# Two convolutional attention layers with group norm on one core: group statistics through small transfers, and a look-ahead that stops at the last phase

## Chip, core and metric

The kernel runs on one core of a Trainium2 chip, in one launch, in fp32 throughout. The metric is the device time in microseconds (us), the median of several executions. Lines such as L428 are lines of the kernel before; the changed kernel has other numbers for the same statements.

## What is computed

Two layers are applied to x of shape (4, 256, 64, 64), each with a residual and each on a group norm of its input. The group norm has 32 groups of 8 channels; each group of one image gets one mean and one variance.

```python
def _gn(v, G=32, eps=1e-5):
    g = v.reshape(B_, G, C_ // G, H_, W_)
    m = jnp.mean(g, axis=(2, 3, 4), keepdims=True)
    s = jnp.var(g, axis=(2, 3, 4), keepdims=True)
    return ((g - m) / jnp.sqrt(s + eps)).reshape(v.shape)
...
x = x + _L0_conv_ref(_gn(x), ...)
x = x + _L1_conv_ref(_gn(x), ...)
```

Layer 0 ("A" in the kernel) is attention with 8 heads of 32 channels, 4096 queries per image and 1024 keys, which come from 2x2 convolutions with stride 2. Layer 1 ("B") is attention within four areas of 1024 positions per image, plus a depthwise 7x7 convolution of the values, plus a 1x1 projection.

## The kernel before

The work is cut into eight blocks: A for the four images, then B for the four images. A block has 16 units (8 chunks of 512 queries times 2 sets of four heads), a unit has 8 steps (128 keys each). The loop at the end of the function goes through 683 **phases**; a phase does one and a half steps. In each phase TensorE makes score products (tile s, L428), ScalarE takes three exponentials of 128x1024 (L469 twice, L480 once, tile p), TensorE multiplies the previous phase's exponentials with the values (tile av, L494), and VectorE adds them up into the tile acc (L504). Tile p has 6 buffers.

All other TensorE work is **side work**: the products for q, k, v, the projection (all through the helper at L167), the convolution (L1048) and the divisors (tile den, L513). It is cut into **parts** by `yield` in generators. A task, made by `task` or `task_at`, says how many parts it has and when it is due. In each phase the loop decides how many parts to put between the scores and the value products: 0, 1, 2 or, when things are late, 4. The decision uses `pressure()` (parts over the time that is left) and `supply()`, a forecast of how many parts per phase will be at hand. `supply()` looks 24 phases ahead, and spreads what it finds at a rate of 13/16 of a phase. Two queues of instructions are of interest besides: GpSimd's, which also issues the small DMAs of the divisors (few, recs, rb: L527, L535, L537), and SP's, which issues all large DMAs. The order on every engine is the one that this Python loop emits; no other scheduler changes it.

Group norm statistics come from `bn_stats` as chunks pass by. When an image's last chunk has been seen, `plan_norm` does the following for its key (`("A", b)` or `("B", b)`): `aggregate` gives mean and variance of each channel, one channel per partition (L346). `means` multiplies them on TensorE by a 128x128 matrix gmat that averages within groups of 8 partitions (tile gm, L351), ScalarE copies the result out (L352), VectorE forms the deviations (L353 to L355). `variances` does a second such product (tile gv, L359), ScalarE adds eps (L360), GpSimd takes the power -0.5 (L363) and makes the shift (L367, L368). Outside the prologue `means` and `variances` don't run at once: `soon` puts them into a queue `quick`, and the loop takes one from it in a phase in which no side work is under way, no unit ends, and none was taken in the two phases before.

```python
        elif quick and not begun() and not cut and f < PHASES and f > quick_at[0] + 2:
            quick.popleft()()
            quick_at[0] = f
        else:
            if rate > 2:
                parts = side_parts(4)
```

So a phase that takes a group product takes no side work: the branches exclude each other. The normalizations that use the result (`normalize`, L390 and L392) are held back until four phases after it was issued (`after`, `known`).

After the last phase the loop drains what is left: the last units' divisors (their reciprocals go from few through a DRAM tile recs into rb), the last projections `project` and `project_last` (tile ops, L167, taken out by L831 and L859 into xm), and the output DMAs (L834, L860). Outside of the prologue every side product takes the same PSUM bank, `ps_side`.

Of the kernel before, what the change touches and what calls it, by code (L numbers as in the profile page):

```python
# [9 lines left out]
FP = mybir.dt.float32  # L10
I32 = mybir.dt.int32
AF = mybir.ActivationFunctionType
ALU = mybir.AluOpType
AX = mybir.AxisListType

P = 128
B, C, HH, WW = 4, 256, 64, 64
N = HH * WW
CT = C // P
# [19 lines left out]
EPS = 1e-5  # L39
# [21 lines left out]
def direct_path(  # L61
# [122 lines left out]
    plan = {}  # L184

    def at(g, j, f):
        g, j = g + int(j // NKT), int(j % NKT)
        plan.setdefault((g, j), []).append(f)

    side, quick, quick_at = deque(), deque(), [-9]
    now, last = [-1], len(BLOCKS) * UNITS * NKT

    phase = [0]
# [17 lines left out]

    def supply():

        far = 24
        comes = [0] * (far + 1)
        chained = 0
        for parts, _, started, ready, _ in side:
            if started or ready is None or ready():  # L220
                comes[0] += parts
            elif ready.__name__ == "chained":
                chained += 5
                comes[min(chained, far)] += parts
            else:
                comes[1] += parts
        for when, parts in upcoming:
            if when - phase[0] <= far:
                comes[max(when - phase[0], 1)] += parts
        total, least = 0, 4.0  # L230
        for h in range(far):
            total += comes[h]
            least = min(least, total / max(1, (h + 1) * 13 / 16))
        return least

    def choose():
# [35 lines left out]
    def begun():  # L272
        return bool(side) and side[0][2]
# [39 lines left out]

        return ready

    def soon(f):

        if now[0] < 0:
            f()
        else:  # L320
            quick.append(f)

    stats, norms = {}, {}

    def stats_of(key):
# [4 lines left out]
    def keep_busy(n):  # L330
        ps = ps_pair("idle")[:, 0, :P]
        for _ in range(n):
            T.matmul(ps, lhsT=idle, rhs=idle, start=True, stop=True)

    def plan_norm(key, g, j):

        name = f"{key[0]}{key[1]}"
        made = {}

        def aggregate():  # L340
            for tag, cols in (("mv", 2), ("gmean", 1), ("dev", 1), ("gvar", 1)):
                shape = [P, CT, cols] if cols > 1 else [P, CT]
                made[tag] = pool.tile(shape, FP, tag=tag, name=f"{tag}_{name}", bufs=2)
            mv = made["mv"]
            for t in range(CT):
                V.bn_aggr(out=mv[:, t, :], in_=stats[key][:, t].rearrange("p c s -> p (c s)"))  # L346

        def means():
            mv, mean, dev = made["mv"], made["gmean"], made["dev"]
            ps = ps_side(f"gm_{name}")[:, :CT]  # L350
            T.matmul(ps, lhsT=gmat, rhs=mv[:, :, 0], start=True, stop=True)  # L351
            S.copy(mean, ps)  # L352
            V.tensor_sub(dev, mv[:, :, 0], mean)  # L353
            V.tensor_mul(dev, dev, dev)
            V.tensor_add(dev, dev, mv[:, :, 1])  # L355

        def variances():
            ps = ps_side(f"gv_{name}")[:, :CT]
            T.matmul(ps, lhsT=gmat, rhs=made["dev"], start=True, stop=True)  # L359
            S.activation(made["gvar"], ps, AF.Identity, bias=eps)  # L360
            norm = pool.tile([P, 2, CT], FP, tag="norm", name=f"norm_{name}", bufs=8)
            shift, rstd = norm[:, 0, :], norm[:, 1, :]
            G.tensor_tensor(rstd, made["gvar"], neghalf, ALU.pow)  # L363
            if key == ("A", 0):
                V.scalar_tensor_tensor(shift, made["gmean"], -1.0, rstd, ALU.mult, ALU.mult)
            else:
                G.tensor_tensor(shift, made["gmean"], rstd, ALU.mult)  # L367
                G.tensor_scalar(shift, shift, -1.0, None, ALU.mult)  # L368
            norms[key] = shift, rstd
            known[key] = phase[0] if now[0] >= 0 else -4  # L370

        def quietly(f, n):
            f()
            if key == ("A", 0):
                keep_busy(n)

        if key == ("A", 0):
            at(g - 1, 0, lambda: keep_busy(44))
        at(g, j, aggregate)
        at(g, j + (2 if g >= 0 else 1), lambda: soon(lambda: quietly(means, 4)))  # L380
        at(g, j + (6 if g >= 0 else 3), lambda: soon(lambda: quietly(variances, 10)))

    def normalize(key, dst, src, t, by_vector=False):
        while key not in norms:
            while begun():
                advance()
            quick.popleft()()
        shift, rstd = norms[key]
        if by_vector:
            V.tensor_scalar(dst, src, rstd[:, t : t + 1], shift[:, t : t + 1], ALU.mult, ALU.add)  # L390
            return
        S.activation(dst, src, AF.Identity, bias=shift[:, t : t + 1], scale=rstd[:, t : t + 1])  # L392
# [763 lines left out]
        task(parts, g, *args, due=0.6)  # L1156
    f = step = 0
    before, credit = [], 0.0
    while f < PHASES or before or plan or side or quick or norms_left or to_add or to_divide:
        now[0], phase[0] = step, f  # L1160
        exps = scores(f) if f < PHASES else [lambda: None] * 3
        mine = []
        if f < PHASES:
            full, half = parts_of(f)
            mine = sorted(([half] if half else []) + [(full, None)], key=lambda b: b[0])
        due = bool(to_divide)
        exps[0]()
        add_ready()
        due = bool(to_divide) if f >= PHASES else due
        exps[1]()  # L1170
        cut = boundary(before)
        for s, u in before[:cut]:
            accumulate(s, u)
        if cut:
            copies[0] += 1
        _, rate = pressure()
        parts = done_den = 0
        wanted = credit + max(min(supply(), 2.0), min(rate, 2.0))
        bare = cut and not begun() and not due and f < PHASES and rate <= 1.5 and (wanted < 0.8 or not choose())
        if cut and not bare:  # L1180
            evict(before[0][0] // NKT)
        exps[2]()
        if bare:
            evict(before[0][0] // NKT)
            banks.reverse()
            credit = min(wanted, 0.5)
        elif due and not begun():
            done_den = 1
            copies[0] += 1
            g = to_divide.popleft()  # L1190
            divisors(g, *([last - 1] if g == final else []))
            if g < final:
                divide(g, units[g])
            else:
                rb = pool.tile([P, CH], FP, tag="p", name="rb", bufs=PB)
                V.reciprocal(rb, dens[g])
                spare.extend((dens.pop(g), rb))
        elif quick and not begun() and not cut and f < PHASES and f > quick_at[0] + 2:
            quick.popleft()()
            quick_at[0] = f  # L1200
        else:
            if rate > 2:
                parts = side_parts(4)
            elif rate > 1.5 or due or f >= PHASES or wanted >= (0.8 if cut else 1.5):
                parts = side_parts(2)
            elif begun() and side[0][0] % 2:
                parts = side_parts(1)
            elif boundary(mine):
                parts = side_parts(2) if wanted >= 0.9 else 0
            elif wanted >= 0.5 and not cut or begun():  # L1210
                parts = side_parts(1)
            credit = max(-0.5, min(wanted - parts, 0.5))
        for s, u in before[cut:]:
            accumulate(s, u)
        add_ready()
        if f >= PHASES:
            side_parts(2)
        if quick and f >= PHASES:
            quick.popleft()()
        while step < -(-3 * (f + 1) // 2):  # L1220
            do(*divmod(step, NKT))
            step += 1
        for _ in range(3):
            load_share()
        if before:
            evict(before[-1][0] // NKT, True)
        work = max(parts, done_den)
        force = f >= PHASES or f < 20 or pressure()[0] <= 4
        while norms_left and (force or busy(work, 0.75) <= 0.3 + 0.1 * len(norms_left)) and norm_next():
            copies[0] += 1  # L1230
            force = f >= PHASES
        behind[0], copies[0] = min(busy(work), 0.4), 0
        if before:
            evict(before[-1][0] // NKT)
        before = mine
        to_add.extend((s, n) for s, u in mine for n in ((0, 1) if u is None else (2 + u,)))
        f += 1
# [597 lines left out]
```

## Time and profile before

| what | us |
|---|---|
| median of 3 executions (3064.57 to 3065.95) | 3065.22 |
| the profiled execution, its own time | 3063.53 |
| its span from first to last instruction | 3061.5 |
| prologue, to the first score product of the loop | 72.06 |
| 682 phases, from the first to the last phase's first score product | 2961.4 |
| last phase and drain, to the end of the span | 28.1 |

The profiled execution is 1.7 us under the median. TensorE's granted clock was 0.998. In the profile PE is TensorE, PEld its weight loads, DVE is VectorE, ACT is ScalarE, POOL is GpSimd, SP is SyncE; a line of the timeline gives start in us, length in us, engine, source line, operation, what is written from what, and how many instructions were merged; in brackets stands the engine's idle time before it and what ended it. An fp32 matmul of the program shows as two records.

### The profile page before, as it was taken

The numbers are of one execution on the slowest core, as the hardware profiler recorded it, in microseconds if no ns is written. First come the engines' busy times: TensorE is split into PE (matmuls) and PEld (weight loads), VectorE is DVE, ScalarE is ACT, GpSimd is POOL, SyncE is SP. The second block draws the span as 40 slices with busy tenths as digits, with TensorE's granted clock in tenths as the row PEclk, the third lists the DMA queues.
The fourth block names the chain that finished last, engine by engine and source line by source line (L and its number), as shares of the span: only waits on it lengthen the run. The fifth ranks groups of instructions, "written<-read, shape, count | busy, mean of one in ns | idle before, by whom it ended". The sixth has DMA issues, their size and how long they took to land.

```text
span 3061.5 us, 108320 instructions
## 1 busy us (share of the span) xinstructions
PE 3032.8 (99%) x47254; PEld 1280.0 (42%) x47254; DVE 2526.2 (83%) x2769; ACT 2455.9 (80%) x2988; POOL 433.8 (14%) x794
## 2 busy tenths in 40 slices
PE   9999999999999999999999999999999999999998
PEld 6444434444344444333444444444434444443332
DVE  3788988889887787878888888788878888888888
ACT  3888888888887888888888877788777787878885
POOL 0011111111111111111111111111111111111111
PEclk9999999999999999999999999999999999999999
DMA  5244533466354557777866677667755565553232
GB/s 191 51 101 98 126 92 73 109 142 165 83 140 133 143 152 175 189 161 194 204 175 162 156 176 185 152 171 178 176 127 145 144 159 143 149 139 79 50 71 62
DMA packets 644250, 422.73 MB, mean 138 GB/s; under 512 B 409740, under 2 KB 552572, under 8 KB 643768
## 3 DMA queue, kind: packets, MB, share of 16 engines
q1 hardware_dynamic: 619384, 380.11, 49.3%
q0 software_dynamic: 24384, 35.62, 5.1%
q8 instruction: 373, 6.11, 0.9%
q14 instruction: 109, 0.89, 0.1%
HBM read 317.28 MB, written 97.05 MB: 135 GB/s over the span
## 4 chain that ended last, share of the span: by engine, by line
PE 91%; DMA 3%; DVE 2%; ACT 2%; issue 2%; SPq 1%; POOL 0%; DVEq 0%; ACTq 0%; POOLq 0%
PE s L428 31%; PE av L494 26%; PE k0ps L167 4%; PE den L513 4%; PE v0ps L167 4%; PE q1ps L167 4%; PE k1ps L167 4%; PE conv_ps L1048 4%; PE q0ps L167 4%; PE ops L167 4%; PE vals_ps L167 3%; DVE acc L504 1%; ACT p L469 1%; DMA vals<-vout 1%; DMA rows<-vals 1%
## 5 line engine op out<-in xcount | busy, mean ns | idle before, releaser
L504 DVE TENSOR_TENSOR acc<-acc,p 128x1024 f32<-128x1024 f32 x1790 | 2117.4, 1220 | 382.7 <-PE av L494 285.7
L469 ACT ACTIVATE p<-s 128x1024 f32<-128x1024 f32 x1194 | 1159.8, 1025 | 419.3 <-PE s L428 407.6
L480 ACT ACTIVATE p<-s 128x1024 f32<-128x1024 f32 x598 | 619.8, 1036 | 1.5 <-DVE acc L504 0.7
L428 PE MATMUL s<-q,k_A 32*64 32x256 f32 (+1 forms) x10928 | 541.1, 494 | 4.1 <-ACT p L469 3.5
L428 PE MATMUL s<-q,k_B 32*64 32x512 f32 (+1 forms) x10912 | 537.1, 494 | 2.8 <-ACT p L469 2.4
L494 PE MATMUL av<-p,v_A 128*32 128x256 f32 (+1 forms) x4784 | 451.4, 486 | 0.0
L494 PE MATMUL av<-p,v_B 128*32 128x512 f32 (+1 forms) x4776 | 449.4, 487 | 0.0
L428 PEld LDWEIGHTS s<-q,k_B 32*64 32x64 f32 x10912 | 266.0, 130 | 325.1 <-PE s L428 60.4
L428 PEld LDWEIGHTS s<-q,k_A 32*64 32x64 f32 x10928 | 263.2, 130 | 329.1 <-PE s L428 58.5
L537 POOL DMA_DIRECT2D rb<-recs x508 | 251.4, 501 | 510.3 <-DMA recs<-few 497.9
L535 POOL DMA_DIRECT2D recs<-few x127 | 71.3, 561 | 1719.9 <-DVE sums L534 1600.3
L494 PEld LDWEIGHTS av<-p,v_B 128*32 128x32 f32 x4776 | 149.2, 110 | 264.5 <-issue 238.3
L494 PEld LDWEIGHTS av<-p,v_A 128*32 128x32 f32 x4784 | 149.5, 110 | 227.5 <-issue 186.0
L469 ACT ACTIVATE acc<-s 128x1024 f32<-128x1024 f32 x172 | 167.0, 1023 | 80.6 <-PE s L428 80.2
L513 PE MATMUL den<-acc,ones 128*32 128x512 f32 x1024 | 138.5, 605 | 0.9 <-DVE xm L831 0.9
L167 PE MATMUL ops<-cv,wp_sb 128*32 128x512 f32 x1024 | 126.6, 605 | 4.7 <-DVE xm L831 3.5
L527 POOL DMA_DIRECT2D few<-den_sb x127 | 90.5, 713 | 271.9 <-ACT den_sb L526 271.3
L167 PE MATMUL vals_ps<-hv,wqkv_sb 128*32 128x512 f32 x1024 | 124.9, 598 | 0.5 <-issue 0.5
L167 PE MATMUL q1ps<-h,wqkv_sb 128*32 128x512 f32 x1024 | 124.9, 599 | 0.0
L167 PE MATMUL k1ps<-h,wqkv_sb 128*32 128x512 f32 x1024 | 123.0, 597 | 1.7 <-ACT cout L1059 0.9
L167 PE MATMUL q0ps<-hq,wq_sb 128*32 128x512 f32 x1024 | 124.0, 597 | 0.1
L167 PE MATMUL k0ps<-taps,wkv 128*32 128x256 f32 x2048 | 123.9, 383 | 0.0
(102 smaller groups left out, 2089.5 us busy)
## 6 DMA issues: line engine op xcount, KB each, us to landing
rows<-vals SPq DMA_DIRECT2D x384, 195.9 KB
rb<-recs POOLq DMA_DIRECT2D x508, 64.0 KB, 3.6
share<-vals SPq DMA_DIRECT2D x128, 195.9 KB
vala<-vout SPq DMA_DIRECT2D x128, 144.0 KB
vals<-vout SPq DMA_DIRECT2D x128, 144.0 KB
vc<-vala SPq DMA_DIRECT2D x64, 288.0 KB
band<-mats SPq DMA_DIRECT2D x96, 176.0 KB
hq<-in_x SPq DMA_DIRECT2D x32, 512.0 KB
```

The source lines that it names most:

```text
L167: T.matmul(out[cols, :], lhsT=lhsT[:, cols], rhs=rhs, start=start, stop=stop)
L428: T.matmul(out[n : n + WIDE], lhsT=unit[2]()[rows, unit[0], j * P + n : j * P + n + WIDE], rhs=unit[1]()[rows, cols], start=True, stop=True,)
L469: S.activation(p, (a, b)[n], AF.Exp, scale=SCALE)
L480: S.activation(p, c.rearrange("p b (l n) -> p b l n", l=2), AF.Exp, scale=SCALE)
L494: T.matmul(out, lhsT=v[:, j, unit[0] * P + HD * h : unit[0] * P + HD * h + HD], rhs=rhs, start=(j == 0 and not u), stop=(j == NKT - 1), sk ...
L504: V.tensor_add(to, to, p)
L513: T.matmul(dens[g][HD * h : HD * h + HD, :], lhsT=ones, rhs=p(h), start=(n == 0), stop=(n == len(sets) - 1),)
L527: G.dma_start(few[:, 0, :], den_sb[0:P:HD, :].rearrange("h (q n) -> h q n", n=CH // HD))
L535: G.dma_start(recs.rearrange("h (q n) -> (h q) n", n=CH // HD), few[:, 1, :])
L537: G.dma_start(rb[HD * h : HD * h + HD, :], recs[h : h + 1, :].to_broadcast([HD, CH]))
L1048: T.matmul(ps[HD * m : HD * m + HD, (2 * k + i) * size : (2 * k + i + 1) * size].rearrange("p (y x) -> p y x", y=NY), lhsT=band[:, half].r ...
```

## The change

For all keys but the first (`("A", 0)`, in the prologue), the two products, the two copies and the deviations go. In their place `gather` issues two DMAs on GpSimd's queue that bring mean and variance of each channel from one channel a partition to one group a partition (a tile of 32 partitions with 8 channels x 2 values); `of_groups` lets VectorE take the statistics of the 8 means, and the sum of the 8 variances; `scatter` makes scale and shift in five small GpSimd operations, and two more DMAs bring them back to every channel's partition. The steps are issued at fixed steps of the plan (1, 5 and 6 steps after `aggregate`; 1, 2 and 3 in the prologue), not through `quick`, which goes with its branch of the loop. The tile norm has 4 buffers in place of 8. `supply()` no longer looks beyond the last phase, and spreads at 14/16 in place of 13/16.

```diff
-    side, quick, quick_at = deque(), deque(), [-9]
+    side = deque()
...
-        far = 24
+        far = max(1, min(24, PHASES - phase[0]))
...
-            least = min(least, total / max(1, (h + 1) * 13 / 16))
+            least = min(least, total / max(1, (h + 1) * 14 / 16))
...
+        def gather():
+            by_group = made["by_group"] = pool.tile([CT * NG, 8, 2], FP, tag="by_group", name=f"by_group_{name}", bufs=1)
+            for t in range(CT):
+                G.dma_start(by_group[t * NG : (t + 1) * NG], made["mv"][:, t, :])
+
+        def of_groups():
+            by_group = made["by_group"]
+            for tag, cols in (("spread", 6), ("of_means", 2), ("within", 1), ("scale", 2)):
+                made[tag] = pool.tile([CT * NG, cols], FP, tag=f"group_{tag}", name=f"{tag}_{name}", bufs=1)
+            V.bn_stats(out=made["spread"], in_=by_group[:, :, 0])
+            V.bn_aggr(out=made["of_means"], in_=made["spread"])
+            V.tensor_reduce(made["within"], by_group[:, :, 1], AX.X, ALU.add)
+
+        def scatter():
+            scale, within, of_means = made["scale"], made["within"], made["of_means"]
+            shift, rstd = scale[:, 0:1], scale[:, 1:2]
+            G.tensor_scalar(within, within, 0.125, EPS, ALU.mult, ALU.add)
+            G.tensor_tensor(within, within, of_means[:, 1:2], ALU.add)
+            G.tensor_tensor(rstd, within, neghalf[: CT * NG, 0:1], ALU.pow)
+            G.tensor_tensor(shift, of_means[:, 0:1], rstd, ALU.mult)
+            G.tensor_scalar(shift, shift, -1.0, None, ALU.mult)
+            norm = pool.tile([P, CT, 2], FP, tag="norm", name=f"norm_{name}", bufs=4)
+            for t in range(CT):
+                G.dma_start(norm[:, t, :], scale[t * NG : (t + 1) * NG].unsqueeze(1).to_broadcast([NG, 8, 2]))
+            norms[key] = norm[:, :, 0], norm[:, :, 1]
             known[key] = phase[0] if now[0] >= 0 else -4
...
-        at(g, j + (2 if g >= 0 else 1), lambda: soon(lambda: quietly(means, 4)))
-        at(g, j + (6 if g >= 0 else 3), lambda: soon(lambda: quietly(variances, 10)))
+        if by_products:
+            at(g - 1, 0, lambda: keep_busy(44))
+            for n, f, more in ((1, means, 4), (3, variances, 10)):
+                at(g, j + n, f)
+                at(g, j + n, lambda more=more: keep_busy(more))
+        else:
+            for n, f in (((1, gather), (5, of_groups), (6, scatter)) if g >= 0 else ((1, gather), (2, of_groups), (3, scatter))):
+                at(g, j + n, f)
...
-        elif quick and not begun() and not cut and f < PHASES and f > quick_at[0] + 2:
-            quick.popleft()()
-            quick_at[0] = f
```

More of the change, by code (lines that the diff above doesn't have):

```diff
@@ L314, in normed @@
         return ready
[L316 to L321, printed above, removed]
     stats, norms = {}, {}
@@ L338, in plan_norm @@
         made = {}
+        by_products = key == ("A", 0)
+        NG = P // 8
         def aggregate():
[L341 to L344, printed above, removed]
+            mv = made["mv"] = pool.tile([P, CT, 2], FP, tag="mv", name=f"mv_{name}", bufs=2)
+            if by_products:
+                for tag in ("gmean", "dev", "gvar"):
+                    made[tag] = pool.tile([P, CT], FP, tag=tag, name=f"{tag}_{name}", bufs=1)
             for t in range(CT):
@@ L360, in variances @@
             S.activation(made["gvar"], ps, AF.Identity, bias=eps)
-            norm = pool.tile([P, 2, CT], FP, tag="norm", name=f"norm_{name}", bufs=8)
-            shift, rstd = norm[:, 0, :], norm[:, 1, :]
+            norm = pool.tile([P, CT, 2], FP, tag="norm", name=f"norm_{name}", bufs=4)
+            shift, rstd = norm[:, :, 0], norm[:, :, 1]
             G.tensor_tensor(rstd, made["gvar"], neghalf, ALU.pow)
[L364 to L368, printed above, removed]
@@ L369, in variances @@
-            norms[key] = shift, rstd
-            known[key] = phase[0] if now[0] >= 0 else -4
[L372 to L377, printed above, removed]
-            at(g - 1, 0, lambda: keep_busy(44))
-        at(g, j, aggregate)
-        at(g, j + (2 if g >= 0 else 1), lambda: soon(lambda: quietly(means, 4)))
-        at(g, j + (6 if g >= 0 else 3), lambda: soon(lambda: quietly(variances, 10)))
+            V.scalar_tensor_tensor(shift, made["gmean"], -1.0, rstd, ALU.mult, ALU.mult)
@@ new lines, in variances @@
+            norms[key] = shift, rstd
+            known[key] = -4
+        def gather():
[9 more added lines that the diff above has]
+            V.tensor_reduce(made["within"], by_group[:, :, 1], AX.X, ALU.add)
@@ new lines, in scatter @@
+        def scatter():
[6 more added lines that the diff above has]
+            G.tensor_scalar(shift, shift, -1.0, None, ALU.mult)
+            norm = pool.tile([P, CT, 2], FP, tag="norm", name=f"norm_{name}", bufs=4)
+            for t in range(CT):
+                G.dma_start(norm[:, t, :], scale[t * NG : (t + 1) * NG].unsqueeze(1).to_broadcast([NG, 8, 2]))
+            norms[key] = norm[:, :, 0], norm[:, :, 1]
+            known[key] = phase[0] if now[0] >= 0 else -4
@@ L383, in normalize @@
+        at(g, j, aggregate)
+        if by_products:
+            at(g - 1, 0, lambda: keep_busy(44))
+            for n, f, more in ((1, means, 4), (3, variances, 10)):
[4 more added lines that the diff above has]
+                at(g, j + n, f)
     def normalize(key, dst, src, t, by_vector=False):
-        while key not in norms:
-            while begun():
-                advance()
-            quick.popleft()()
@@ L1158, in direct_path @@
     before, credit = [], 0.0
-    while f < PHASES or before or plan or side or quick or norms_left or to_add or to_divide:
+    while f < PHASES or before or plan or side or norms_left or to_add or to_divide:
         now[0], phase[0] = step, f
@@ L1197, in direct_path @@
                 spare.extend((dens.pop(g), rb))
-        elif quick and not begun() and not cut and f < PHASES and f > quick_at[0] + 2:
-            quick.popleft()()
-            quick_at[0] = f
         else:
@@ L1217, in direct_path @@
             side_parts(2)
-        if quick and f >= PHASES:
-            quick.popleft()()
         while step < -(-3 * (f + 1) // 2):
```

## The prediction

> **What bounds the kernel now.** I read the page's busy times first, then the timeline of PE alone, since the busy shares don't separate the engines.
>
> ```profile
> PE 3032.8 (99%) x47254; PEld 1280.0 (42%) x47254; DVE 2526.2 (83%) x2769; ACT 2455.9 (80%) x2988; POOL 433.8 (14%) x794
> ...
> PE 91%; DMA 3%; DVE 2%; ACT 2%; issue 2%; SPq 1%; POOL 0%; DVEq 0%; ACTq 0%; POOLq 0%
> ```
>
> PE is busy all the time and has 91% of the chain that ended last;[...] so I look for its pace.
>
> ```profile
> 486.99 1.55 PE L428 MATMUL s<-q,k_A 32*64 32x256 f32 x32
> 488.47 1.93 PE L167 MATMUL v0ps<-wkv,taps 128*32 128x256 f32 x32
> 490.22 1.47 PE L494 MATMUL av<-p,v_A 128*32 128x512 f32 x16
> 491.62 1.55 PE L428 MATMUL s<-q,k_A 32*64 32x256 f32 x32
> 493.10 0.38 PE L351 MATMUL gm_B<-mv_B,gmat 128*128 128x2 f32 x2
> 493.41 1.50 PE L494 MATMUL av<-p,v_A 128*32 128x256 f32 x16
> 494.84 1.96 PE L428 MATMUL s<-q,k_A 32*64 32x256 f32 x32
> 496.73 1.92 PE L167 MATMUL q0ps<-hq,wq_sb 128*32 128x512 f32 x16
> ...
> 499.87 1.55 PE L428 MATMUL s<-q,k_A 32*64 32x256 f32 x32
> ...
> 504.52 1.55 PE L428 MATMUL s<-q,k_A 32*64 32x256 f32 x32
> 505.99 1.07 PE L513 MATMUL den<-acc,ones 128*32 128x512 f32 x8
> ...
> 508.28 1.54 PE L428 MATMUL s<-q,k_A 32*64 32x256 f32 x32
> ```
>
> Each burst of s opens a phase. With two parts (486.99 to 491.62) a phase lasts 4.63 us, with one (504.52 to 508.28) 3.76. Over all 682 phases, with parts counted from the order of the instructions, the medians are 3.76 for one and 4.62 for two: **2.895 us + 0.865 us a part**, PE's own pace. A phase without parts should then take 2.90, but takes 3.17 to 3.22 (491.62 to 494.84), because ACT's three exponentials need 3.1; and the next phase runs late too: 494.84 to 499.87 is 5.03 in place of 4.62, its scores taking 1.96 in place of 1.55. So an **empty phase costs 0.28 + 0.46 = 0.74 us** (0.28, 0.46, 0.28 for two in a row), and the parts it didn't take cost their 0.865 elsewhere.
>
> Before has 42 empty phases, 1088.8 parts. Pace: 682 x 2.895 + 1088.8 x 0.865 = 2916.2; measured 2961.4; the excess of 45.2 us is all that any spreading can win. Of it the empty phases make 29.0 by this rule. About 8 lie near phases 270 to 330 (1.2 to 1.46 ms), where ACT and DVE wait for the tile vout behind stores and loads on SP's queue; the rest is scattered.
>
> **The end is another stage.** From 2985 us (phase 668) DVE has no idle time but for tenths until it waits for rb at 3041.45:
>
> ```profile
> 3024.08 10.81 DVE L504 TENSOR_TENSOR acc<-acc,p 128x1024 f32<-128x1024 f32 x9
> 3035.41 0.24 DVE L533 RECIPROCAL few<-few 128x16 f32<-128x16 f32 x1
> 3043.02 0.69 DVE L540 TENSOR_TENSOR att_B<-av_sb,rb 128x512 f32<-128x512 f32 x1 [1.57 <-DMA rb<-recs]
> 3044.43 0.20 PEld L167 LDWEIGHTS ops<-cv,wp_sb 128*32 128x32 f32 x8 [3.96 <-DVE xm L831]
> 3045.27 3.33 DVE L1196 RECIPROCAL rb<-den 128x512 f32<-128x512 f32 x1
> 3054.96 0.75 DVE L831 SCALAR_TENSOR_TENSOR xm<-ops,bproj_sb,xm 128x512 f32<-128x512 f32 x1 [0.80 <-PE ops L167]
> ```
>
> There the end follows the order on DVE, not PE's pace.
>
> [...] few<-den_sb, 8 KB, takes 4.3 us from issue to landing, recs 3.8. [...] PE waited 3.96 us for xm.
>
> **The change, part by part.** The order of the changed program counts what moves; durations are the trace's.
>
> 1. *Group products leave.* 12 of the 42 empty phases are those that hold gm or gv (six keys, two each; A1's pair stands in the prologue and in phase 0). With the transfers alone in place 29 are left: these 12 are filled, and one more by regrouping. Up to phase 668, where PE sets the pace, the rule gives 25.7 us before and 16.6 after (with all edits): **-9.1**. The parts done by then are the same.
> 2. *Their own time*: an empty phase with a product is 0.04 longer (3.22 for 3.17): 12 x 0.04 = **-0.5**. At phase 0 the gv product splits the scores: they begin at 72.06 and resume at 73.02, **-0.9**.
> 3. *The transfers.* Two issues of 0.7 each (L527's mean)[...]. On POOL they stand after few and before recs, where POOL idles for 1600 us in all (waits for sums). DVE reaches the group statistics 9 to 12 adds of 1.22 later: by the matching adds of before, 11.1 us for A2, 12.5 B0, 15.3 A3, 11.6 B1. **0**, with 5 us to spare; behind the waiting DVE stand the reciprocal of few and all adds. In the prologue aggregation ends near 44.2, and k_A's next add starts at 51.12 after 6.92 idle: 0.
> 4. *DVE's small operations*: three of at most 0.34 (bn_aggr of 48[...]) for three of 0.16: 7 x 0.5 at most, off PE's path. **0**. ACT loses 14 copies of 0.18 to 0.28: 0.
> 5. *POOL's five operations*: by L363, L367, L368 pow 1.2 to 1.3, the others 0.3 to 1.2, 2.9 to 4.9 us, then two issues, 1.4; behind them stands few, whose result DVE takes some 8 to 20 us later. 0. After the statistics come recs (0.56, 2.7 to 3.8), four rb (2.0), these (up to 6.3) and the landing (4.3): at most 17.5. The nearest user is A3's taps in phase 164, 16.6 after the matching add; A2 and B0 have 22 and 23. **0 to +1**; I take 0. The four buffers of norm suffice: no more than four keys are in use at once.
> 6. *14/16*: with all else, it moves empty phases but leaves 29 at 29: 0.3 us by the rule, inside step 1.
> 7. *Look-ahead*: 29 becomes 26, all three after phase 668 (676, 677, 680, 681 go, 678 comes). ops_5_1's two parts move from the drain into phases 680 and 681. Their 1.73 us of PE are no gain where DVE sets the pace, and their xm (0.75) now stands on DVE ahead of the last few: +0.75 on the chain few, recs, rb. After att_B, DVE does 0.66 + 1.04 + 3.18 + 0.06 before the last att now (7.2 us to the end of cv); then it will be rb 3.3, cv 1.1, xm 0.75, a wait of 1.9 for ops_6_1 in the same bank, xm 0.75, att 0.7, cv 1.1 = 9.6: +2.4. Against that ops_6_1 no longer comes last (1.9 of PE and its xm: the last xm ends 3055.71, L859's 3054.16, -1.55), and the last output is 256 KB where it was 512: 0 to -1.5. Sum 0.75 + 2.4 - 1.55 = +1.6, less that: 0.1 to 1.6. I take **+1.0**.
>
> Sum: -9.1 - 0.5 - 0.9 + 1.0 = **-9.5**. Profiled 3063.5 gives 3054.0; the median lies 1.7 above it, so 3065.2 - 9.5 = **3055.7**. The forecast's own range is 3051 to 3059: 1 us for step 5, 1 for step 7, the rest for how stalls on SP's queue fall.
>
> **Rivals.**
> *B, the vout stalls ease too.* The value tasks in phases 270 to 330 move by one to three phases. For: their 8 us hang on where stores and loads meet on SP's queue. Against: the order puts the same loads (share, band, rows) in phases 290 to 292 (291 to 293 before) and the same stores behind them. 3055.7 - 7.8 = 3047.9.
> *C, they swallow the gain.* Here DMA would set the time: PE arrives earlier and waits longer. Up to phase 289 the rule has won 5.3 us; lost, that leaves 3061.0. For: DMA is 73% busy from 1250 to 1700 us. Against: the chain shows DMA for two short stretches only.
> *D, slower: the gather lands late.* Place: DVE at the group statistics, six times in the loop, with all adds behind it. Price: each us beyond the spacing of 11. The gain is gone at 11 + 9.5 / 6 = 12.6 us, slower by 0.2% from 13.6; at 15 it is 3055.7 + 24 = 3080. For: 128 pieces of 8 bytes, which no row shows. Against: few's 4.3 us.
>
> **How the numbers follow.** About 0.2% (6.1 us) can be told from no change: faster is under 3059.1. Forecast 0.62, B 0.13, C 0.19, D 0.06. C lies within 0.2%, D is slower; the forecast's upper edge gives 0.02 to "same". So faster 0.73, same 0.21, slower 0.06. The range 3047.5 to 3061.5 leaves out D, a third of C, and the low end of B, 0.16 in all.
>
> **What would show it.** PE's timeline has no empty phases at the keys (near phases 77, 100, 160, 185, 271, 356), and about 26 in all; the phases keep 3.76 and 4.62. DVE shows no idle time before the statistics of by_group; ACT none at the first taps of A3. The last instructions are L859's successor and its output. Wrong it would be if DVE's idle time ended by by_group passes a few us, if waits for vout grow beyond 8 us, or if the drain is over 30 us.

## The result, and the profile after

The changed kernel takes 3078.5 us (median of 6 executions, 3067.7 to 3084.2) where the kernel before takes 3065.6 on the same chip: ratio **1.0040, 95% interval 1.0027 to 1.0053**, slower by 0.4%. A second series on another chip gave 1.0028 (1.0016 to 1.0041). The forecast was 3055.7.

The profile after is of its fastest execution (3067.7 us, span 3065.9). First the page's busy times and the first line of its chain:

```profile
PE 3020.5 (99%) x47226; PEld 1290.9 (42%) x47226; DVE 2524.5 (82%) x2769; ACT 2454.8 (80%) x2974; POOL 449.3 (15%) x836
...
PE 90%; DMA 3%; DVE 2%; ACT 2%; issue 2%; SPq 1%; POOL 0%; ACTq 0%; DVEq 0%; POOLq 0%
```

These look like before: PE has 28 matmuls less and as many weight loads less, POOL 42 instructions more. Nothing in them tells that the time rose. The stretch of PE's timeline that held an empty phase with a group product:

```profile
481.87 1.55 PE L441 MATMUL s<-q,k_A 32*64 32x256 f32 x32
...
486.50 1.55 PE L441 MATMUL s<-q,k_A 32*64 32x256 f32 x32
...
491.12 1.55 PE L441 MATMUL s<-q,k_A 32*64 32x256 f32 x32
...
495.74 1.55 PE L441 MATMUL s<-q,k_A 32*64 32x256 f32 x32
...
500.38 1.55 PE L441 MATMUL s<-q,k_A 32*64 32x256 f32 x32
...
505.01 1.55 PE L441 MATMUL s<-q,k_A 32*64 32x256 f32 x32
...
508.77 1.55 PE L441 MATMUL s<-q,k_A 32*64 32x256 f32 x32
```

Phases of two parts last 4.62 to 4.64 us, one of one part 3.76, and the empty phase is gone: the pace law of the prediction holds. So I took the time apart by it: over the 682 phases, what is beyond 2.895 + 0.865 a part is split into empty phases and the rest, **stalls**. The column of empty phases is their number and the rule's price for them, not a measurement of its own. "Last 26" is phases 656 to 681; the two last columns are from the start of the last phase to the end of the last xm on DVE, and from there to the end of the program. All are us of one profiled execution; the ratio is of all executions.

| kernel | ratio (95%) | empty phases | stalls, phases 120-160 | 250-330 | others | last 26 | to last xm | after it |
|---|---|---|---|---|---|---|---|---|
| before | 1 | 42: 28.7 | 0.4 | 8.4 | 7.7 | 100.8 | 22.3 | 5.8 |
| full change | 1.0040 (1.0027-1.0053) | 26: 18.8 | 4.7 | 17.0 | 6.8 | 102.3 | 21.2 | 10.1 |
| again (e1) | 1.0028 (1.0016-1.0041) | 26: 18.8 | 6.4 | 13.0 | 7.1 | 102.3 | 23.6 | 9.9 |
| transfers alone (e2) | 0.9979 (0.9969-0.9988) | 29: 19.2 | 0.0 | 8.4 | 7.1 | 100.9 | 22.2 | 8.6 |
| both supply edits alone (e3) | 1.0050 (1.0036-1.0063) | 41: 28.5 | 3.7 | 8.0 | 10.6 | 102.3 | 23.7 | 7.1 |
| transfers + 14/16 (e5) | 1.0035 (1.0022-1.0049) | 29: 19.5 | 5.8 | 27.6 | 6.4 | 100.7 | 22.1 | 8.2 |
| transfers + look-ahead (e6) | 1.0008 (1.0000-1.0016) | 26: 18.5 | 0.0 | 11.4 | 8.5 | 102.4 | 24.0 | 10.2 |
| look-ahead alone (e12) | 1.0018 (1.0012-1.0025) | 39: 27.9 | 0.4 | 9.4 | 10.0 | 102.4 | 24.6 | 6.9 |

The full change against before, by profile: empty phases -9.9, two parts more +1.7, stalls +12.0, end -1.1 + 4.4, and -2.7 ahead of phase 0 (PE's clock had fallen to 0.5 there for 6.8 us in the profile of before): +4.4, as the spans (3065.9 - 3061.5). The gain came, and was lost elsewhere. This profile is of the shortest of the six executions and holds 4.4 of the 12.9 us between the medians. The other five executions had a granted clock of 0.993 or 0.994 in place of its 0.997; from this I estimate some 18 to 25 us more at half clock in each of them.

Where? The largest stall is at phase 302. PE's timeline:

```profile
1376.39 1.55 PE L441 MATMUL s<-q,k_A 32*64 32x256 f32 x32
1377.86 1.07 PE L167 MATMUL vals_ps<-hv,wqkv_sb 128*32 128x512 f32 x8
1378.75 1.47 PE L507 MATMUL av<-p,v_A 128*32 128x256 f32 x16
1386.71 2.90 PE L441 MATMUL s<-q,k_A 32*64 32x256 f32 x32 [6.49 <-ACT p L482]
```

PE waits 6.49 us for ACT, and then the same burst of scores takes 2.90 in place of 1.55: the clock is at 0.5 from 1383.8 for 10.2 us. ACT, DVE and SP's queue there:

```profile
1384.03 0.81 ACT L405 ACTIVATE hq<-hq,norm_A 128x512 f32<-128x512 f32 x1 [7.36 <-DMA hq<-in_x]
```

```profile
1389.83 0.07 DVE L976 MEMSET vout<- 128x16 f32 x1 [10.73 <-DMA vals<-vout]
```

```profile
1369.49 2.82 SPq L1045 DMA_DIRECT2D rows<-vals  x4
1372.65 0.60 SPq L108 DMA_DIRECT2D hq<-in_x  x1
1374.76 0.35 SPq L968 DMA_DIRECT2D hv<-xmid  x1
1375.38 1.86 SPq L993 DMA_DIRECT2D vala<-vout  x2
1377.69 6.65 SPq L1001 DMA_DIRECT2D vals<-vout  x2
1384.45 3.50 SPq L993 DMA_DIRECT2D vala<-vout  x2
```

ACT waits for a load, issued at 1372.65 in a row of loads and stores without a gap and landed at 1384.0; DVE waits for a store of vout. On SP even the issue takes long here: the two stores of vals in the row of 6.65 us took 1.79 and 4.74. The trace's records also show at what SP's queue stood still. Its 2132 transfers name eight semaphores in a fixed turn, and 403 of their issues (444 in before) started within 0.05 us of a landing of the transfer eight places ahead, which names the same one, after waits of 284 us in all (303 in before). The load of hq at 1372.65 is one of them: it started 0.01 us after the landing of a load of share that was issued at 1366.76. So is the first store of vals in the row of 6.65 us, 0.02 us after the landing of a load of rows issued at 1369.49. Of the 403, 17 are stores of vout behind another transfer (10.1 us), and 9 are other transfers behind a store of vout (6.2 us). In the order of the waits the same places stand out (us in total, times, longest):

```profile
DVE vout L976 <- DMA vals<-vout: 19.7, 5, 10.7
DVE st_A L577 <- DMA xs<-in_x: 8.6, 4, 4.2
ACT hq L405 <- DMA hq<-in_x: 7.4, 1, 7.4
```

Before:

```profile
DVE vout L963 <- DMA vals<-vout: 6.5, 2, 4.7
DVE st_A L564 <- DMA xs<-in_x: 3.9, 3, 3.0
ACT hq L392 <- DMA hq<-in_x: 2.0, 1, 2.0
```

In the loop no wait of DVE for by_group is among them: the gathers landed after 1.7 to 6.9 us. In the drain (DVE):

```profile
3047.26 0.72 DVE L844 SCALAR_TENSOR_TENSOR xm<-ops,bproj_sb,xm 128x512 f32<-128x512 f32 x1
3050.03 0.75 DVE L844 SCALAR_TENSOR_TENSOR xm<-ops,bproj_sb,xm 128x512 f32<-128x512 f32 x1 [2.05 <-PE ops L167]
...
3055.06 0.73 DVE L872 SCALAR_TENSOR_TENSOR xm<-ops,bproj_sb,xm 128x512 f32<-128x512 f32 x1
```

The order is the predicted one; the program ends 10.1 us after the last xm, where before ended 5.8 after it.

### The profile page after: what moved, and what is told of

It reads as the page before. It is cut to its first block, busy times and chain, and to the rows that moved or that the text cites. A ratio compares the mean times of both kernels' runs of the same rounds, so it can differ in the third digit from the quotient of the medians.

```text
span 3065.9 us, 108357 instructions
## 1 busy us (share of the span) xinstructions
PE 3020.5 (99%) x47226; PEld 1290.9 (42%) x47226; DVE 2524.5 (82%) x2769; ACT 2454.8 (80%) x2974; POOL 449.3 (15%) x836
## 4 chain that ended last, share of the span: by engine, by line
PE 90%; DMA 3%; DVE 2%; ACT 2%; issue 2%; SPq 1%; POOL 0%; ACTq 0%; DVEq 0%; POOLq 0%
PE s L441 31%; PE av L507 26%; PE conv_ps L1061 4%; PE q1ps L167 4%; PE den L526 4%; PE k1ps L167 4%; PE q0ps L167 4%; PE k0ps L167 4%; PE v0ps L167 4%; PE ops L167 3%; PE vals_ps L167 3%; DVE acc L517 1%; ACT p L482 1%; DMA vals<-vout 1%; DMA hq<-in_x 0%
## 5 line engine op out<-in xcount | busy, mean ns | idle before, releaser
L441 PE MATMUL s<-q,k_A 32*64 32x256 f32 (+1 forms) x10928 | 537.8, 495 | 11.6 <-ACT p L482 10.5
```

Of the source, the lines that this page charges most:

```text
L441: T.matmul(out[n : n + WIDE], lhsT=unit[2]()[rows, unit[0], j * P + n : j * P + n + WIDE], rhs=unit[1]()[rows, cols], start=True, stop=True,)
```

## The experiments

My first theory was rival C with more weight: transfers and supply edits alike bring PE to SP's queue earlier, and the queue takes the gain back. The rivals: the transfers cost the time; the supply edits cost it.

**e1, the change again**, unchanged.

> The changed kernel once more, unchanged. Theory (the pace gain is real but is lost where SP's in-order DMA queue sets the time, near phases 145 to 153 and 280 to 320, and each long stall of PE there can drop its clock for about 10 us): again 3067 to 3084 us, and a profile of a typical execution shows longer stalls at those places than the one at hand, with more than one stretch at half clock. Rival 1 (the small transfers, or what waits for them, cost the time): DVE or POOL idle time ended by by_group or norm of 10 us or more in the typical execution. Rival 2 (chance differences between chips): below 3066 here.

3068.9 us (3065.3 to 3072.5), ratio 1.0028. Same places, but 19.4 us of stalls there, where I had expected more than the 21.7 of the first profile; three half-clock stretches (702.0, 1384.7, 3047.0) and one at the end. The interval is above 1 on this chip too: the loss is the kernel's.

**e2, the transfers alone**: the full change with 13 / 16 and `far = 24`.

```diff
-        far = max(1, min(24, PHASES - phase[0]))
+        far = 24
-            least = min(least, total / max(1, (h + 1) * 14 / 16))
+            least = min(least, total / max(1, (h + 1) * 13 / 16))
```

> The group transfers alone, with 13/16 and a look-ahead of 24 as before. Theory (stalls on SP's queue swallow the gain): the loads and stores near phases 145 and 300 fall much as in the full change, so 3062 to 3078 us, with the stalls again at those places. Rival 1 (the transfers cost it): the same time as the full change or more, 3070 to 3082, with the cost spread over the six keys. Rival 2 (the supply edits cost it): the forecast's gain without the drain, 3054 to 3058.

3053.2 us where before takes 3060.1 on this chip, ratio 0.9979: **faster by 0.2%**. My theory fell in this point; "the supply edits cost it" came nearest, with 3054 to 3058. There are no stalls in phases 120 to 160, and 2.8 us more after the last xm. The 682 phases take 2951.1 us where before takes 2961.4: -10.3.

**e3, the supply edits alone**: the same two lines changed in the kernel before.

> The kernel before with the two supply edits alone (14/16, and look-ahead that ends at the last phase), group products kept. Theory (stalls on SP's queue): the edits move value tasks by few phases; 3060 to 3072 us, with 2 to 4 us of it in the drain. Rival 1 (the transfers cost it): within 3 us of the kernel before. Rival 2 (the supply edits cost it): 3072 to 3082.

3076.1 us, ratio 1.0050, as rival 2 has it. Without a single transfer, all of the loss is there, and stalls in phases 120 to 160 with it.

**e4, the share's five loads on GpSimd's queue**, in the full change.

```diff
-        nc.sync.dma_start(band, mats[k])
+        nc.gpsimd.dma_start(band, mats[k])
...
-            nc.sync.dma_start(
+            nc.gpsimd.dma_start(
```

> The changed kernel with the five loads of every share (band and four of rows) issued from GpSimd's queue in place of SyncE's. Theory (stalls on SP's queue): stores of vout and loads of hq no longer stand behind them; the waits for vout and hq near phases 280 to 320 shrink from about 27 us to under 8, there is no stretch at half clock near 1384 us, and the time falls by 8 to 20 us, to 3055 to 3068. Rival 1 (the small transfers cost it): no fall, or a rise, since POOL's queue now holds more: 3075 to 3090. Rival 2 (the supply edits): no change, within 3 us of the changed kernel.

3074.2 us, ratio 1.0047: a miss, no fall but a rise over e1. The waits for vout did go (2.0 and 1.4 us), and the stall at 302; but one of 9.0 came at phase 295:

```profile
POOL band L1042 <- PE conv_ps L1061: 165.2, 32, 15.1
DVE few L546 <- DMA few<-den_sb: 22.5, 5, 12.1
```

Loads that wait for a buffer now block GpSimd's queue, and few, which DVE needs, stands behind them. The run moved the wait and says nothing of its cause.

**e5 and e6, one supply edit each**, with the transfers: e5 has `far = 24`, e6 has 13 / 16.

> The changed kernel with the look-ahead of 24 as before: transfers and 14/16. Theory (14/16 alone sets value tasks up to four phases later, so that stores of vout fall among runs of loads on SP's queue): nearly all of the loss is here, 3062 to 3070 us, with stalls near phases 145 to 155 and 300 as in the full change. Rival (the look-ahead costs it, in the drain): 3053 to 3057, near the transfers alone.

> The changed kernel with 13/16: transfers and the look-ahead that ends at the last phase. Theory (14/16 costs it): 3053 to 3057 us, no stalls near phases 145 to 155; the drain up to its last xm is 1 to 2 us longer than that of the transfers alone. Rival (the look-ahead costs it): 3062 to 3070.

e5: 3075.6 us, 1.0035, more than the theory's bounds. e6: 3067.1 us, 1.0008, which lies in the rival's range and not in the theory's. Added to the transfers alone, 14/16 costs 0.56% and the look-ahead 0.29% (from ratios of different chips). Taken out of the full change (1.0040 and 1.0028), 14/16 is worth 0.20 to 0.32%, the look-ahead nothing that can be told. 14/16 is the larger both ways, as the theory had it. e5's profile is of an execution at 3078.5 us, as long as the full change's first median; it may show what such a one holds: stalls of 7.6 at phase 283, 6.1 and 5.1 at 302 and 303, 3.8 at 315, and four stretches at half clock between 700 and 1460 us. Its waits:

```profile
DVE vout L976 <- DMA vals<-vout: 28.0, 7, 10.5
ACT vout L988 <- DMA vals<-vout: 17.0, 4, 7.9
```

The traces show what 14/16 moved. The numbers are phases: for a vout, the phase in which SP issued the first of the four stores, for each of the two halves; for loads, the phase of the issue.

| | before | transfers, 13/16 (e2) | transfers, 14/16 (e5) | e9: 14/16, due 3 | e10: 13/16, due 5 |
|---|---|---|---|---|---|
| stores of vout_0_1 | 123, 127 | 122, 123 | 126, 127 | 118, 120 | 122, 123 |
| stores of vout_0_2 | 129, 132 | 127, 129 | 131, 132 | 128, 129 | 127, 129 |
| stores of vout_0_3 | 138, 142 | 138, 142 | 142, 143 | 133, 137 | 146, 147 |
| loads xs_3_3 to xs_3_5 (among those of made_30, made_31) | 141 to 146 | 141 to 146 | 141 to 147 | 141 to 145 | 142 to 147 |
| stores of vout_1_7 | 289, 291 | 287, 289 | 288, 290 | 283, 287 | 288, 291 |
| first share of batch 1 | 292 | 289 | 291 | 287 | 292 |

With 14/16 the forecast of supply is lower, so value tasks start later, up to four phases. In phases 120 to 160 both halves of vout_0_3 then stand among loads whose place is fixed by the plan; with 13/16 the first half is clear of them. For phases 250 to 330 the table has no such answer: before has vout_1_7 and the first share as late as any, and 8.4 us of stalls.

**e7, the transfers alone, issued from SyncE's queue.**

```diff
-                G.dma_start(by_group[t * NG : (t + 1) * NG], made["mv"][:, t, :])
+                nc.sync.dma_start(by_group[t * NG : (t + 1) * NG], made["mv"][:, t, :])
...
-                G.dma_start(norm[:, t, :], scale[t * NG : (t + 1) * NG].unsqueeze(1).to_broadcast([NG, 8, 2]))
+                nc.sync.dma_start(norm[:, t, :], scale[t * NG : (t + 1) * NG].unsqueeze(1).to_broadcast([NG, 8, 2]))
```

> The transfers alone (13/16, look-ahead of 24), with the gather and scatter issued from SyncE's queue in place of GpSimd's. Theory (GpSimd's DRAIN at the end of the program takes longer for the transfers that its queue issued, 4.2 to 4.4 us in place of 1.7): it takes 1.7 again, and the time is 2 to 3 us lower than that of the transfers alone, 3050 to 3051.5. Rival 1 (the DRAIN does not hang on them): no change in it, 3052 to 3054. Rival 2 (they stand behind loads on SP's queue and come late): waits for by_group or norm of 5 us and more in the loop, 3056 to 3070.

3056.4 us where before takes 3065.4 on this chip: 0.9975 (0.9968 to 0.9983), not the theory's 3050 to 3051.5. After the last xm 5.4 us in place of 8.6, and GpSimd's DRAIN is 1.71 again: the theory's size, but 5.1 us of waits for by_group came, as rival 2 has it, and the ratio alone doesn't tell 0.9975 from 0.9979. e13 and e14 do.

**e8, the four stores of each vout issued from ScalarE's queue**, in the full change (`nc.sync` to `nc.scalar` in both loops of stores).

> The full change with the four stores of each vout issued from ScalarE's queue in place of SyncE's. Theory (with 14/16 these stores meet runs of loads on SP's queue): waits for vout fall under 5 us, stalls in phases 120 to 160 from 5 to under 2 and in 250 to 330 from 13 to 17 to under 8, and the time by 8 to 14 us, to 3054 to 3061. Rival 1 (not the queue, but the order of PE's parts or DMA's own load): no fall. Rival 2 (256 issues on ScalarE lie in PE's path): slower, over 3075.

3322.7 us, 1.0841: rival 2, and how. ScalarE's timeline:

```profile
682.10 1.10 ACTq L993 DMA_DIRECT2D vala<-vout  x2
685.83 4.55 ACTq L1001 DMA_DIRECT2D vals<-vout  x2
690.43 0.81 ACT L405 ACTIVATE hv<-hv,norm_B 128x512 f32<-128x512 f32 x1 [8.36 <-DMA made<-bands]
```

The row of 4.55 is two issues of 0.36 and 0.37 with 3.8 us between them, and the profile has the 8.36 us in which ScalarE computes nothing end with the landing of a transfer of SP, made<-bands. Of 256 issues, 25 came after such a wait, 37 us in all, and the issues themselves took 224 us, 0.36 to 5.4 each. Both lie in PE's path. The run says nothing on 14/16.

**e9 and e10, the place of the value tasks, and so of their stores.** e9 keeps 14/16 and lets value tasks fall due a group earlier; e10 keeps 13/16 and lets them fall due a group later. Both have the transfers and `far = 24`.

```diff
-                when + 7, 2, values, t, due=start + 4,
+                when + 7, 2, values, t, due=start + 3,
```

> Transfers and 14/16 (look-ahead of 24), with the due time of the value tasks one group earlier (start + 3 in place of start + 4): the stores of vout_0_3 then stand at phases 132 and 137, as clear of the run of matrix loads at 141 to 146 as with 13/16, and those of batch 1 up to six phases ahead of the shares. PE's empty phases stay at 30. Theory (14/16 costs time only through where these stores meet loads on SP's queue): stalls in phases 120 to 160 under 1 us in place of 5.8, in 250 to 330 under 15 in place of 27.6; ratio to before 0.996 to 1.000. Rival (14/16 costs it in another way, through PE's pace): ratio stays at 1.003 or more.

> Transfers alone (13/16, look-ahead of 24), with the due time of the value tasks one group later (start + 5): the stores of vout_0_3 fall at phases 144 and 145, among the matrix loads. Theory (place on SP's queue): stalls of 3 to 7 us in phases 120 to 160, where the transfers alone have none, and 2 to 8 more in 250 to 330; ratio to before 1.000 to 1.004. Rival (14/16 costs it in another way): no stall there, ratio 0.997 to 0.999.

e9: 3060.9 us, **0.9989** (0.9981 to 0.9997); stalls 2.2 and 13.7, where 14/16 alone has 5.8 and 27.6. e10: 3076.6 us, **1.0038** (1.0025 to 1.0050); stalls 8.4 and 20.8, where the transfers alone have 0.0 and 8.4. Both ratios are the theory's (the stalls of e9 in 120 to 160 and both of e10 are above its bounds), and the rival's are excluded: 14/16 is fast with the value tasks elsewhere, and 13/16 slow with them there. The edits move the tasks' products on PE with the stores; that the stores do it is argued from what the waits end with. The waits of e10:

```profile
ACT vout L988 <- DMA vals<-vout: 18.0, 3, 13.7
DVE vout L976 <- DMA vals<-vout: 15.5, 2, 11.4
DVE st_A L577 <- DMA xs<-in_x: 13.0, 3, 6.6
```

And of e9:

```profile
ACT vout L988 <- DMA vals<-vout: 10.3, 2, 5.9
DVE vout L976 <- DMA vals<-vout: 7.6, 2, 4.9
DVE st_A L577 <- DMA xs<-in_x: 1.7, 2, 1.1
```

The wait for xs, the load beside vout_0_3, is 1.3 us in e2 and 7.8 in e5.

**e11, a third buffer for vout**, one less for vc, with e5's order.

```diff
-            vout = pool.tile([P, RC, TX, XT], FP, tag="vout", name=f"vout_{b}_{c}_{t}", bufs=2)
+            vout = pool.tile([P, RC, TX, XT], FP, tag="vout", name=f"vout_{b}_{c}_{t}", bufs=3)
...
-            vcs[a, n] = pool.tile([P, 2, 4 * TX, XT], FP, tag="vc", name=f"vc_{b}_{a}_{n}", bufs=4)
+            vcs[a, n] = pool.tile([P, 2, 4 * TX, XT], FP, tag="vc", name=f"vc_{b}_{a}_{n}", bufs=3)
```

> Transfers and 14/16 with the same order of instructions, but three buffers for vout in place of two (and three for vc in place of four, for the room). Theory (the stalls of phases 250 to 330 are waits for vout's stores to leave SP's queue): waits for vout under 3 us, stalls in 250 to 330 under 12 us in place of 27.6; those in 120 to 160, which wait for loads, stay at 4 to 6; ratio to before 0.998 to 1.001. Rival 1 (the loads are late whatever vout does: hq, hv and rows end the waits instead): stalls stay over 20, ratio 1.003. Rival 2 (the fourth vc was needed): new waits for vc from phase 365 on, ratio over 1.003.

3081.1 us, 1.0048, not the theory's 0.998 to 1.001. The waits for vout are gone, all 45 us, and stalls in 250 to 330 fell from 27.6 to 13.9; what is left there ends with a load. Those in 120 to 160 stayed (6.2). But 18.9 us of new stalls came, in phases 422 to 526, where conv_ps waits for loads of the shares:

```profile
ACT hq L405 <- DMA hq<-in_x: 8.1, 1, 8.1
PE conv_ps L1061 <- DMA rows<-vals: 4.0, 3, 1.7
PE conv_ps L1061 <- DMA share<-vals: 2.3, 1, 2.3
```

So in phases 250 to 330 about half of the stalls left with the third buffer, and the other half did not. That the loss of the fourth vc delays the queue, as rival 2 has it, fits the ratio, but no wait for vc itself is in the trace: it is not shown.

**e12, the look-ahead alone**, in the kernel before.

> The kernel before with the look-ahead that ends at the last phase, nothing else. Theory (it moves two parts from the drain into the last phases and so makes both longer): the last phase starts 1.5 to 2 us later, the drain is 1 to 3 longer, all before phase 658 is the same: 3 to 5 us, ratio 1.001 to 1.0016. Rival (it costs 7 to 9 us, as the comparison of the runs without 14/16 and without both hints): ratio 1.002 to 1.003. Rival (nothing or a gain): ratio 0.999 to 1.0005.

3069.8 us where before takes 3063.5: 1.0018 (1.0012 to 1.0025), between the theory and its rival. Last 26 phases +1.6, to the last xm +2.3, after it +1.1: 5.0.

**e13 and e14, a better version.** 13/16, `far = 24`, value tasks due a group earlier, and the transfers on SyncE's queue (e13) or GpSimd's (e14), with the same order on PE, DVE and ACT.

> Transfers alone (13/16, look-ahead of 24), issued from SyncE's queue, with the due time of the value tasks one group earlier (start + 3). PE has 26 empty phases, 2 us less by the rule than with start + 4, and the stores of vout stand clear of the matrix loads. Theory (the loss was the place of the stores on SP's queue and the end of GpSimd's queue; both are avoided here): ratio to before 0.994 to 0.997, the lowest of all. Rival (any other order meets other loads): stalls of over 15 us in phases 250 to 330, ratio 0.997 to 1.000.

> The same with the transfers on GpSimd's queue: the same order of instructions on PE, DVE and ACT. Theory (the transfers on GpSimd's queue lengthen its DRAIN at the end of the program by 2.6 us and what precedes that by 0.6): 2 to 4 us slower than the one on SyncE's queue, all of it after the last xm. Rival (the DRAIN differs for another reason): no difference.

e13: **3053.7 us where before takes 3064.4: 0.9964** (0.9950 to 0.9978), the lowest of all, though its interval meets those of e2 and e7. e14: 3057.5, 0.9979 (0.9972 to 0.9986). The medians of the pair differ by 3.8 us; in the profiles the stretch after the last xm differs by 3.2 (5.6 and 8.8): the theory. e14 also tells what 14/16 costs with the value tasks due a group earlier: e9 is 0.10% above it, where e5 is 0.56% above e2 (ratios of different chips again). So most of the cost of 14/16 is the place of these tasks. e13 still has 18.3 us of stalls in phases 250 to 330 (6.9 at 323), which is what its rival named; so it isn't free of the queue, only of some of its places.

## Why the prediction was wrong, by its steps

- **Steps 1 and 2 (group products leave) were right.** Together they gave -9.1 - 0.5 - 0.9 = -10.5 us; e2's phases take 10.3 less. Of this 0.9 is phase 0: it lasts 6.01 us in before, e3 and e12, and 5.07 in every run with the transfers.
- **Step 3 (transfers in time) was right, but for one instruction outside the steps**: no wait in the loop with the transfers on GpSimd in the profile of the full change, so rival D fell. Its 5 us to spare are 11.1 us between the matching adds, less two issues of 0.7 and few's median landing of 4.3 in before, where few took 2.1 to 8.3. DVE's three new operations take 0.15, 0.17 and 0.12 us, within the sizes of step 4. But after the program's last work, GpSimd has two operations of its own whose length differed with what its queue had issued (durations in us from the trace's records):

| | INC_SWDGE_SEM | DRAIN |
|---|---|---|
| before, e3, e12 | 0.60 to 0.61 | 1.71 |
| transfers on GpSimd's queue (full change, e1, e2, e5, e6, e8 to e11, e14) | 1.23 to 1.27 | 4.24 to 4.40 |
| transfers and share loads on it (e4) | 2.27 | 8.49 |
| transfers on SyncE's queue (e7, e13) | 0.60 to 0.61 | 1.71 |

That is +2.8 to +3.2 us, and no step counted it. This DRAIN is the first of GpSimd's three at the end; the two others take 0.11 and 0.04 us in before and in the full change alike.
- **Step 6 (14/16) failed, and it is the largest part of the loss.** I priced it by its empty phases alone ("it moves empty phases but leaves 29 at 29: 0.3 us by the rule"). It also moves the value tasks, and every one of them has four stores on SP's queue. Cost: 0.56% by e5 over e2, some 17 us, or 0.20 to 0.32% by the full change over e6, some 6 to 10 us; e9, e10 and e14 show that most of it comes with the place of these tasks. The changed program's own order has the move of four phases (vout_0_1, vout_0_2); I looked at shares in phases 290 to 293 only, and not at 120 to 160.
- **Step 7 (look-ahead, +1.0) was mis-sized**: e12 measures +5.5 (3.7 to 7.7 by its interval), though in the full change nothing of it can be told apart. The +0.75 on the chain to few is there. But the two parts moved do cost their 1.6 in the last 26 phases, which I held to be hidden by DVE; xm's wait for ops_6_1 is 2.05 here and 3.51 in e1, where PE's clock falls at 3047; and "the last output is 256 KB where it was 512: 0 to -1.5" has the wrong sign, since GpSimd's last operations begin 3.2 us after the last xm, where e2 has 1.9 and before 1.2. (The 3.96 us that the prediction gives as PE's wait for xm is the idle time of its weight loads; PE's own gap there is 3.05.)
- **Rival C** named the right queue ("PE arrives earlier and waits longer"), but not the edit, and bounded the loss by the gain. Two things break the bound: stores that move to another place lose more than they won, and a stall costs more than its length (phases 302 and 303 of the full change lose 10.7 us, of which PE's gaps are 7.4, and the clock is at 0.5 from 1383.8 for 10.2 us). In these runs the half-clock stretches in the loop lasted 3.4, 6.8, 10.2 or 13.7 us. Gaps of 1.5 to 2.5 us between PE's instructions came before stretches of 3.4 us in e1, e3, e4, e5 and e10. But 1.55 us in the full change (at 699.5) and 2.05 in e6 (at 1385.7) had no such stretch after them, so in these runs the length of the gap alone doesn't decide it.
- **The prediction's own signs of being wrong came true**, two of three: waits for vout of 23.7 us (19.7 of DVE, 4.0 of ACT; 10.4 before) where 8 was the bound, and a drain of 31.3 where 30 was. They point to SP's queue and to the end. Slower had a chance of 0.06, all of it for rival D, which did not happen.

What stays open: 14/16, look-ahead and transfers add up to about +0.6%, while the full change has +0.28 and +0.40; stalls fall differently with each order, so the parts aren't additive, and I can't say of a single stall why it is 6 us and not 2, nor which store and load meet in phases 250 to 330. Keeping PE's clock up during a stall was not tried.

## What to carry to other kernels

A knob that only spreads work also moves all that the work issues: follow its DMAs through their queue, at each place where the queue is full, before pricing it by the engine's pace. Where two edits come together, price and run each alone; here the transfers alone won 0.2% and the two small edits alone lost 0.5%. And ask which queue small transfers leave on: moved from GpSimd's to SyncE's, and with stores clear of the loads, the same idea gives 0.9964.

## What the runs showed of the hardware

- GpSimd's DRAIN at the program's end: 1.71, 4.2 to 4.4 or 8.5 us with what its queue had issued (e7, e14, e4).
- A PE gap of 1.5 us (e3, at 1384.7) was followed by 3.4 us at half clock, one of 12.4 (e10, at 1383.1) by 13.7; one of 2.05 (e6, at 1385.7) by none.
- Issuing a store of vout took the issuing engine 0.36 to 5.4 us on ScalarE (e8), and 1.79 and 4.74 for two on SyncE at 1377.7 (full change).
